# Moving loads, sums and a score spread in a two-layer graph kernel on one core

## The chip, the core and the metric

The kernel runs on one core of a Trainium2 chip. The metric is device time in microseconds (us) of one launch. A core has five engines that run their own instruction streams and wait for each other by semaphores: TensorE (PE in the profile, with its weight loads as PEld), VectorE (DVE), ScalarE (ACT), GpSimd (POOL) and SyncE (SP). Here SP only issues DMA transfers; GpSimd issues some of them too, and adds. All engines work on SBUF; matrix products land in the eight PSUM banks `a1, b1, c1, e1` (set 1) and `a2, b2, c2, e2` (set 2).

## What is computed

128 graphs of 128 nodes with 512 features each, all in float32, go through two layers. Cut to what matters:

```python
h = relu(layernorm(x))
# layer 0
Xw = h @ Wv + bv;  sj = Xw @ aw[:d, 0];  si = Xw @ aw[d:, 0]
e = leaky_relu(sj[:, None, :] + si[:, :, None] + ab[0], 0.2)
t = adj * exp(e);  t = t / (sum(t, -1) + 1e-12)
H = 0;  Xk = h
for k in range(3):
    H = H + Xk @ Wk[k] + bk[k]
    Xk = t @ Xk
x1 = x + relu(H)
# layer 1
h = relu(layernorm(x1))
q, k = split(h @ Wqk);  v = h @ Wv1
w = sum(q * (adj @ (k * mask)), -1) * mask / sqrt(512)
out = x1 + softmax(w, over the nodes)[:, :, None] * v
```

The query and key weights are folded into one matrix beforehand, so layer 1 needs two products of h: one for the score and one for v.

## The kernel before

Layer 0 takes two graphs at a time (64 pairs `p`). Its products are done by a Strassen scheme with seven products instead of eight (`strassen`). In one iteration stand: `y10(p)` (the products with Wk[1] and Wk[0], into set 1), `inner` and `outer` (the multiplications by the transition matrix and the sum x1), `y2(p + 2)` (the product with Wk[2], into set 2), `norm2(p)` (layer 1's norm, sent through DRAM to be transposed by 32x32 blocks), and, inside `y10`, `between`: the norm of x three pairs ahead and the transposes and left sums two pairs ahead (`begin`).

`behind(what, op, ...)` places an instruction after a named earlier one in its engine's stream without a wait of its own.

```python
def load_x(p, queue=nc.sync):
    xg[p] = loads.tile([P, G, D], FP, name="xg")          # 4 buffers
    queue.dma_start(xg[p], x[p * G:(p + 1) * G].rearrange("b n d -> n b d"))
...
def strassen(banks, left, right, s, first, ends, steps={}, gate="warm"):
    ...
    product(a, 1, first);  nc.scalar.copy(b, a)
    product(e, 5, first);  done["s"] = behind(gate, nc.scalar.copy, s[:, 0], e).ins
    product(b, 6);         done["u2"] = behind("s", nc.scalar.copy, c, b).ins
    product(a, 2);         ends[0, 0](a)
    product(c, 7);         nc.scalar.copy(s[:, 1], c);  ends[1, 1](e, s[:, 1])
    product(b, 3);         ends[0, 1](b, s[:, 0])
    product(c, 4);         ends[1, 0](c)
...
for p in range(NP):
    def between():
        ...
        if p + 2 < NP:
            behind("t", begin, p + 2)
        if p + 3 < NP:
            behind("left", norm0, p + 3)
    if p > 1:
        behind("x1", attention, p)
    y10(p, {1: between, 6: lambda: t_transposed(p)})
    if p > 0:
        behind("c12", for_layer1, p - 1)
    ...
    z = inner(p)
    if p == 0:
        y2(1); begin(2); spread_columns(1); behind("left", attention, 1)
    behind("c12" if p else "left", outer, p, z)           # ends with x1's store on SP
    ...
    if p + 2 < NP:
        y2(p + 2)
    ...
    norm2(p)                                              # h2d store and hv loads on SP
    if p + 4 < NP:
        load_x(p + 4)
    if p + 3 < NP:
        load_adj(p + 3)
    if p == 2:
        rightl = behind("x1", combine, ...)               # layer 1's weight sums, 4 large
    if 3 <= p < 3 + len(FACTORS):
        behind("x1", prepare, FACTORS[p - 3], stage)      # 4 small and their stores
```

In `y10` the ends of blocks (1,1) and (0,1) are DVE additions into PSUM (L85 in the profile), placed behind `rs`, the last result of the norm's statistics.

Layer 1 takes four graphs at a time (32 quads `q`). A Strassen scheme is used inside another: seven outer factors of seven products each, done in rounds of one or two factors. `put` and its forms `dve, act, pool, sync, swdge` keep each engine's stream in program order; `swdge` is a DMA issued by GpSimd.

```python
def spread_scores(col):
    t = small.tile([P, S32], FP, name="pwt", bufs=1)
    dve(nc.vector.transpose, t, col)
    d = dram.tile([S32, Q, S32], FP, name="pwd")
    sync(d.rearrange("g q b -> q g b"), t)
    dst = back[3].tile([P, 2 * G, N], FP, name="pw")
    sync(dst.rearrange("p g n -> p (g n)"), bcast(d, 0, 2 * G * N))
    return dst
...
def add_x1(q, pair):                                      # adds x1 to the values while loading
    swdge(values(q, pair), X1D[2 * q + pair].rearrange("g n d -> n g d"), accum_op=OP.add)
...
def catch_up(q):
    if q + 1 < NQ:
        load_left(q + 1, sync)
    scores(q - 1, 1, C[q - 1][:, 2])
    PW[q - 1] = spread_scores(W[q - 1])
    if q > 1:
        add_x1(q - 2, 0)

def last_block(q):                                        # block C22 of the outer scheme
    pool(nc.gpsimd.tensor_add, outer(q, 1), outer(q, 3), outer(q, 1))
```

`scores` multiplies and sums on DVE (the tile `junk`), the scores go through DRAM to be spread over all partitions (`pwd`, `pw`), then DVE takes the peak, ACT the exponentials and DVE the factors of the softmax; ACT scales the values with them.

The last quad (q = 31; prior = 30, late = 29):

```python
together(one_round(q, set1, (1, 6), ...), one_round(q, set2, (2, 7), ...),
         {2: lambda: scale(late, 1, 0), 3: lambda: scale(late, 1, 1), 4: prior_peaks,
          5: prior_factors, 6: lambda: [scale(prior, 0, j) for j in range(G)]})
add_x1(late, 1)
add_x1(prior, 0)
dve(nc.vector.tensor_add, outer(q, 3), outer(q, 3), outer(q, 1))
dve(nc.vector.tensor_add, outer(q, 1), outer(q, 0), outer(q, 1))
aggregate(q)                                              # four PE groups, ACT copies to agg
for j in range(G):
    scale(prior, 1, j)
add_x1(prior, 1)
for at in ((late, 0), (late, 1), (prior, 0), (prior, 1)):
    store(*at)
scores(q, 0, c[:, 2])
# then r4, r5, r3: rounds of one factor, interleaved, with the last quad's own softmax
```

Of the kernel before, what the change touches and what calls it, by code (L numbers as in the profile page):

```python
# [1 line left out]

# [13 lines left out]
def kernel(  # L16
# [32 lines left out]
    G = 2  # L49
# [400 lines left out]
    def attention(p):  # L450

        a, y, pz = ag.pop(p), Y2[p], PZ.pop(p)
        z = front.tile([P, G, N], FP, name="z", bufs=1)
        for j in range(G):
            nc.vector.tensor_scalar(z[:, j, :], pz[:, j, :], y[:, j, 1, HD:], cz, op0=OP.add, op1=OP.add)  # L455
        nc.vector.scalar_tensor_tensor(z, z, 0.2, z, op0=OP.mult, op1=OP.max)
        done["z"] = nc.scalar.activation(z, z, AF.Exp).ins
        d = small.tile([P, 2, G], FP, name="d")
        for j in range(G):
            nc.vector.scalar_tensor_tensor(z[:, j, :], z[:, j, :], 1.0, a[:, j, :], op0=OP.mult,  # L460
                                           op1=OP.mult, accum_out=d[:, 0, j:j + 1])
        nc.vector.tensor_scalar(d[:, 0], d[:, 0], 1e-12, None, op0=OP.add)
        nc.vector.reciprocal(d[:, 1], d[:, 0])
        t = T[p] = front.tile([P, G, N], FP, name="t", bufs=1)
        for j in range(G):
            done["t"] = nc.vector.tensor_scalar(t[:, j, :], z[:, j, :], d[:, 1, j:j + 1], None,
                                                op0=OP.mult).ins
        aT = front.tile([P, G, N], FP, name="aT", bufs=1)
        nc.vector.transpose(aT.rearrange("p g n -> p (g n)"),  # L469
                            agb.pop(p).rearrange("p g q i -> p (g q i)"))  # L470
        for j in range(G):
            b = p * G + j
            behind("z", nc.scalar.activation, aT[:, j, :], aT[:, j, :], AF.Copy, scale=maskT[:, b:b + 1])
        nc.sync.dma_start(ATD[p], aT)
# [59 lines left out]

    RWD = {o: dram.tile([P, 7, HD], FP, name=f"rwd{o}", bufs=1) for o in FACTORS}
# [90 lines left out]
# [3 lines that stand above are left out]
                behind("t", norm0, 2)  # L629
                behind("rs", begin, 1)  # L630
                return
            if p + 2 < NP:
                behind("t", begin, p + 2)
            if p + 3 < NP:
                behind("left", norm0, p + 3)

# [12 lines left out]
        if p == 0:  # L649
            y2(1)  # L650
            begin(2)
            spread_columns(1)
            behind("left", attention, 1)
        behind("c12" if p else "left", outer, p, z)
        if p == 0:
# [11 lines left out]
        if p + 4 < NP:  # L667
            load_x(p + 4)
        if p + 3 < NP:
            load_adj(p + 3)  # L670
        if p == 2:
            rightl = behind("x1", combine, {(kh, k): rl[:, kh * HC:(kh + 1) * HC, k] for kh in range(2)
                              for k in range(2)}, [tl[:, i] for i in range(4)])
        if 3 <= p < 3 + len(FACTORS):
            behind("x1", prepare, FACTORS[p - 3], stage)
# [152 lines left out]
    def spread_scores(col):  # L828
# [5 lines left out]
        sync(d.rearrange("g q b -> q g b"), t)  # L834
        dst = back[3].tile([P, 2 * G, N], FP, name="pw")
        sync(dst.rearrange("p g n -> p (g n)"), bcast(d, 0, 2 * G * N))
# [35 lines left out]
    def catch_up(q):  # L872

        if q + 1 < NQ:
            load_left(q + 1, sync)
        scores(q - 1, 1, C[q - 1][:, 2])
        PW[q - 1] = spread_scores(W[q - 1])
        if q > 1:
            add_x1(q - 2, 0)

    def last_block(q):

        pool(nc.gpsimd.tensor_add, outer(q, 1), outer(q, 3), outer(q, 1))
# [11 lines left out]
    EARLY, LATE = FACTORS[:4], FACTORS[4:]  # L895
    sums = inner_sums(0, LATE)
# [59 lines left out]
    last_block(prior)  # L956
    soft = {}

    def prior_peaks():
        soft[0] = peaks(W[prior], PW.pop(prior))  # L960
        exp_own(*soft[0])
        for j in range(2):
            exp(*soft[0], j)

    def prior_factors():
        for j in range(2, 2 * G):
            exp(*soft[0], j)
        factors(*soft[0])
# [6 lines left out]
             {2: lambda: scale(late, 1, 0), 3: lambda: scale(late, 1, 1), 4: prior_peaks,  # L975
              5: prior_factors, 6: lambda: [scale(prior, 0, j) for j in range(G)]})
    add_x1(late, 1)
    add_x1(prior, 0)

    dve(nc.vector.tensor_add, outer(q, 3), outer(q, 3), outer(q, 1))  # L980
    dve(nc.vector.tensor_add, outer(q, 1), outer(q, 0), outer(q, 1))
    aggregate(q)
    for j in range(G):
        scale(prior, 1, j)
    add_x1(prior, 1)
    for at in ((late, 0), (late, 1), (prior, 0), (prior, 1)):
        store(*at)
    scores(q, 0, c[:, 2])

# [4 lines left out]
    r5 = one_round(q, set2, (5,), s2, plain_ends(lambda i, j: c[:, 2:3, i, j]))  # L994
# [16 lines left out]

    def steps(*order):
        for round, i in order:
            round[i]()

    steps((r4, 0), (r4, 1), (r5, 0), (r4, 2), (r5, 1), (r4, 3))
# [6 lines left out]
    steps((r4, 6))  # L1023
    scores(q, 1, c[:, 0])
# [7 lines left out]

    dve(nc.vector.tensor_add, outer(q, 1), outer(q, 1), outer(q, 2))
    exp(*soft[1], 1)
    dve(nc.vector.tensor_add, outer(q, 3), outer(q, 3), outer(q, 2))
    factors(*soft[1])
    steps((r3, 3), (r3, 4))
    finish(1, 0, c[:, 3, 0], nc.sync)
    steps((r3, 5))
    finish(1, 1, c[:, 3, 1], nc.scalar)  # L1040
    finish(0, 0, c[:, 1, 0], nc.sync)
# [27 lines left out]
```

## Time and profile before

| | |
|---|---|
| time, median of 3 | 2317.68 us (2314.05 to 2321.01) |
| span of the profiled run | 2333.3 us |
| PE busy | 2247.4 us (96%) |
| DVE busy | 1679.4 us (72%) |
| ACT busy | 1254.2 us (54%) |
| POOL busy | 690.4 us (30%) |
| DMA moved | 507.77 MB, mean 218 GB/s |

In the profile `L90` is the line that issues nearly every matrix product and `L554` the helper through which layer 1 issues its work, so in layer 1 an instruction is told by its tiles, written `out<-in`. A square bracket at a line's end tells how long the engine was idle before it and what ended the idling. Layer 0 runs to about 1510 us, layer 1 from there, and the last quad's end from about 2270.

### The profile page before, as it was taken

The page shows a single profiled execution, that of the slowest core. Times are in us where ns is not written, and L with a number is a line of the kernel's source. Part 1 is how long each engine was busy: PE and PEld are TensorE (multiplying, and loading weights), DVE is VectorE, ACT ScalarE, POOL GpSimd, SP SyncE. Part 2 cuts the span into 40 slices and gives each one's busy share as a digit, 9 for nine tenths or more (in the row PEclk, how much of TensorE's full clock was granted, in tenths as well). Part 3 has the DMA queues.
Part 4 walks back from the last instruction along what each step waited for, and adds up shares of the span by engine and source line. Part 5 has one row for each costly group of instructions (what it writes and reads, how often), then busy time and mean ns, then how long its engine had stood idle before and what let it go on. Part 6 is the DMA issues. An engine that isn't in the chain of part 4 may idle for free.

```text
span 2333.3 us, 28894 instructions
## 1 busy us (share of the span) xinstructions
PE 2247.4 (96%) x8227; PEld 1549.4 (66%) x8227; DVE 1679.4 (72%) x4466; ACT 1254.2 (54%) x2932; POOL 690.4 (30%) x787
## 2 busy tenths in 40 slices
PE   8899999999999999999999999999999999999996
PEld 5565655666665665666656566578877878878774
DVE  5577667676766766667666676578877878878776
ACT  3445554554555555455555455446665656656664
POOL 2112111211211211121121121245555555555552
PEclk9999999999999999999999999999999999999998
DMA  8577686766767766666676675768787878878886
GB/s 211 151 240 250 200 265 204 234 200 205 236 200 206 241 202 195 212 217 201 212 225 201 205 241 172 257 207 233 225 237 221 237 222 236 236 216 233 239 221 159
DMA packets 343502, 507.77 MB, mean 218 GB/s; under 512 B 33178, under 2 KB 198426, under 8 KB 326958
## 3 DMA queue, kind: packets, MB, share of 16 engines
q1 hardware_dynamic: 302060, 382.40, 52.9%
q0 software_dynamic: 40992, 123.00, 19.6%
q8 instruction: 65, 1.06, 0.2%
q14 instruction: 95, 0.78, 0.1%
q10 hardware_dynamic: 290, 0.53, 0.1%
HBM read 289.62 MB, written 216.18 MB: 217 GB/s over the span
## 4 chain that ended last, share of the span: by engine, by line
PE 55%; DMA 18%; DVE 15%; ACT 8%; issue 2%; SPq 1%; POOL 1%; DVEq 0%; POOLq 0%; ACTq 0%
PE c L90 16%; PE a L90 15%; PE b L90 14%; DMA xg<-in_x_dram 9%; PE e L90 9%; ACT h L305 4%; DMA pw<-pwd 3%; DMA pwd<-pwt 3%; DVE junk L554 3%; DVE st L281 2%; DVE c L554 1%; DVE s L554 1%; DMA h2d<-h 1%; DVE wcol L554 1%; DVE fw L411 1%
## 5 line engine op out<-in xcount | busy, mean ns | idle before, releaser
L554 POOL TENSOR_TENSOR c<-s,c 128x512 f32<-128x512 f32 (+1 forms) x186 | 200.0, 1090 | 377.8 <-DVE s L554 372.9
L110 POOL DMA_DIRECT2D agb<-in_adj_dram x256 | 150.2, 592 | 531.8 <-DVE aT L469 407.4
L90 PE MATMUL a<-r,x 128*128 128x512 f32 x512 | 243.6, 598 | 3.6 <-ACT a L487 3.5
L554 DVE SCALAR_TENSOR_TENSOR junk<-agg,wscale,c 128x512 f32<-128x512 f32 x128 | 198.0, 1547 | 30.9 <-POOL c L554 25.6
L90 PE MATMUL b<-rw,in 128*128 128x256 f32 x896 | 216.2, 381 | 1.2 <-ACT b L554 1.2
L90 PEld LDWEIGHTS b<-rw,in 128*128 128x128 f32 x896 | 171.1, 191 | 25.7 <-ACT b L554 2.3
L554 POOL TENSOR_TENSOR c<-c 128x1024 f32<-128x1024 f32 x62 | 159.4, 2572 | 2.9 <-DVE c L554 0.7
L281 DVE BATCH_NORM_STATS2 st<-xg 128x6 f32<-128x512 f32 x128 | 82.3, 685 | 82.4 <-DMA xg<-in_x_dram 81.8
L90 PEld LDWEIGHTS a<-r,x 128*128 128x128 f32 x512 | 93.2, 192 | 69.7 <-issue 62.5
L90 PE MATMUL c<-t,x 128*128 128x512 f32 x256 | 125.2, 612 | 13.7 <-ACT s L385 13.3
L90 PE MATMUL a<-w,x 128*128 128x257 f32 x512 | 132.3, 380 | 3.1 <-DVE z L455 3.1
L90 PE MATMUL b<-w,sx 128*128 128x257 f32 x512 | 132.6, 381 | 0.0
L554 ACT ACTIVATE c<-c,wcol 128x512 f32<-128x512 f32 x124 | 86.2, 720 | 83.3 <-DVE wcol L554 83.3
L85 DVE TENSOR_TENSOR e<-e,s 128x512 f32<-128x512 f32 x64 | 44.7, 698 | 119.9 <-ACT s L385 119.9
L305 ACT ACTIVATE h<-xg,rs 128x512 f32<-128x512 f32 x128 | 97.2, 806 | 56.8 <-DVE rs L293 56.7
L90 PE MATMUL c<-rw,in 128*128 128x256 f32 x448 | 110.7, 387 | 16.9 <-ACT c L554 16.9
L377 ACT COPY b<-a 128x257 f32<-128x257 f32 (+1 forms) x128 | 59.5, 465 | 123.4 <-PE a L90 120.6
L90 PE MATMUL c<-t,sx 128*128 128x512 f32 x256 | 121.3, 596 | 2.3 <-ACT c L85 2.1
L90 PE MATMUL b<-t,sx 128*128 128x512 f32 x256 | 120.6, 593 | 0.0
L90 PE MATMUL b<-r,sx 128*128 128x512 f32 x256 | 120.3, 592 | 0.0
L90 PE MATMUL e<-t,sx 128*128 128x512 f32 x256 | 120.3, 592 | 0.0
L90 PE MATMUL a<-rw,f 128*128 128x256 f32 x448 | 108.9, 382 | 9.7 <-ACT agg L554 9.4
(243 smaller groups left out, 5172.5 us busy)
## 6 DMA issues: line engine op xcount, KB each, us to landing
fd<-fw POOLq DMA_DIRECT2D x62, 1024.0 KB, 6.7
x1d<-x SPq DMA_DIRECT2D x64, 512.0 KB, 7.0
h2d<-h SPq DMA_DIRECT2D x64, 512.0 KB, 3.5
hv<-h2d SPq DMA_DIRECT2D x256, 128.0 KB, 3.8
f<-fd SPq DMA_DIRECT2D x32, 1024.0 KB, 9.4
xg<-in_x_dram SPq DMA_DIRECT2D x63, 512.0 KB, 4.7
hd<-h SPq DMA_DIRECT2D x63, 512.0 KB, 3.1
hv<-hd SPq DMA_DIRECT2D x252, 128.0 KB, 2.9
```

Source lines behind the costliest of these rows:

```text
L85: return op(*args, **how)
L90: done["mm"] = op(*args, **how).ins
L110: nc.gpsimd.dma_start(agb[p][c * S32:(c + 1) * S32].rearrange("p g q i -> p (g q) i"), v[c])
L281: nc.vector.bn_stats(st, src[:, j, :])
L305: nc.scalar.activation(to, at, AF.Relu, bias=rs[:, 1, j:j + 1], scale=rs[:, 0, j:j + 1])
L377: nc.scalar.copy(b, a)
L411: nc.vector.transpose(blocks[:, k, j].rearrange("p f (n b) -> p f n b", n=Q), hv[:, j].rearrange("p n (k f a) -> p k f n a", k=2, f=HC)[:, k])
L554: done[engine] = op(*args, **how).ins
```

## The change

The change moves work; the arithmetic is the same but for who does it at the end.

- In layer 0, `load_x(p + 4)` is issued right behind x1's store, ahead of norm2's store and loads in SP's stream. It is for having x in SBUF when the statistics want it.
- Layer 1's weight sums (`combine`, `prepare`) leave the place ahead of attention and go behind the norm's statistics in `between`.
- In the first iteration, attention's first step (z) goes ahead of `begin(2)`.
- In layer 1, the score spread is issued by GpSimd instead of SP, the accumulation of x1 ahead of it, and block C22 waits, by way of a copy of one column into `gate`, for DVE's inner sums of the next quad. It is for letting DVE's scores run without GpSimd's addition beside them.
- At the end, the prior quad's softmax goes behind `aggregate`, its values are scaled on ACT, added to a loaded copy of x1 (`xp`) on GpSimd, and stored from there (`finish_scaled`); the sums with factor 5's product go to GpSimd in pieces, and one of the four last finishes goes to ACT and GpSimd.

```diff
-    def attention(p):
+    def attention(p, early_work=None):
...
-            nc.vector.tensor_scalar(z[:, j, :], pz[:, j, :], y[:, j, 1, HD:], cz, op0=OP.add, op1=OP.add)
-        nc.vector.scalar_tensor_tensor(z, z, 0.2, z, op0=OP.mult, op1=OP.max)
+            done["pz"] = nc.vector.tensor_scalar(z[:, j, :], pz[:, j, :], y[:, j, 1, HD:], cz,
+                                                 op0=OP.add, op1=OP.add).ins
+        if early_work:
+            behind("pz", early_work)
+        behind("left" if early_work else "pz", nc.vector.scalar_tensor_tensor, z, z, 0.2, z, op0=OP.mult, op1=OP.max)
...
@@ between()
                 behind("left", norm0, p + 3)
+            if p == 2:
+                rightl.update(behind("rs", combine, ...))
+            if 3 <= p < 3 + len(FACTORS):
+                behind("rs", prepare, FACTORS[p - 3], stage)
...
             y2(1)
-            begin(2)
             spread_columns(1)
-            behind("left", attention, 1)
+            attention(1, lambda: begin(2))
         behind("c12" if p else "left", outer, p, z)
+        if p + 4 < NP:
+            load_x(p + 4)
...
         norm2(p)
-        if p + 4 < NP:
-            load_x(p + 4)
         if p + 3 < NP:
             load_adj(p + 3)
-        if p == 2:
-            rightl = behind("x1", combine, ...)
-        if 3 <= p < 3 + len(FACTORS):
-            behind("x1", prepare, FACTORS[p - 3], stage)
...
@@ spread_scores
-        sync(d.rearrange("g q b -> q g b"), t)
+        swdge(d.rearrange("g q b -> q g b"), t)
         dst = back[3].tile([P, 2 * G, N], FP, name="pw")
-        sync(dst.rearrange("p g n -> p (g n)"), bcast(d, 0, 2 * G * N))
+        swdge(dst.rearrange("p g n -> p (g n)"), bcast(d, 0, 2 * G * N))
...
@@ catch_up
             load_left(q + 1, sync)
+        if q > 1:
+            add_x1(q - 2, 0)
         scores(q - 1, 1, C[q - 1][:, 2])
         PW[q - 1] = spread_scores(W[q - 1])
-        if q > 1:
-            add_x1(q - 2, 0)

     def last_block(q):

+        if q + 2 < NQ:
+            o = LATE[0]
+            pool(nc.gpsimd.tensor_copy, gate, IN[q + 1, o][:, 3, :1])
         pool(nc.gpsimd.tensor_add, outer(q, 1), outer(q, 3), outer(q, 1))
...
@@ the last quad
     last_block(prior)
+    xp = back[3].tile([P, 2, G, D], FP, name="xp")
+    for i in range(2):
+        sync(xp[:, i], X1D[2 * prior + i].rearrange("g n d -> n g d"))
...
-             {2: lambda: scale(late, 1, 0), 3: lambda: scale(late, 1, 1), 4: prior_peaks,
-              5: prior_factors, 6: lambda: [scale(prior, 0, j) for j in range(G)]})
+             {2: lambda: scale(late, 1, 0), 3: lambda: scale(late, 1, 1)})
     add_x1(late, 1)
-    add_x1(prior, 0)
...
+    soft[2] = peaks(W[prior], PW.pop(prior))
     aggregate(q)
-    for j in range(G):
-        scale(prior, 1, j)
-    add_x1(prior, 1)
-    for at in ((late, 0), (late, 1), (prior, 0), (prior, 1)):
-        store(*at)
+    exp_own(*soft[2])
+    for j in range(2 * G):
+        exp(*soft[2], j)
+    for pair in range(2):
+        store(late, pair)
     scores(q, 0, c[:, 2])
+    factors(*soft[2])
...
+    def sum_of_p5(end):
+        def both(*args, at):
+            end(*args)
+            for to in (1, 3):
+                pool(nc.gpsimd.tensor_add, c[:, to, at[0], at[1]], c[:, to, at[0], at[1]], c[:, 2, at[0], at[1]])
+        return both
...
+    def finish_scaled(quad, pair, graphs, at, r):
+        w = 3 * 2 * G + pair * G
+        for j in range(graphs.start, graphs.stop):
+            v = C[quad][:, at, j].rearrange("p h d -> p (h d)")
+            act(nc.scalar.activation, v, v, AF.Copy, scale=W[quad][:, w + j:w + j + 1])
+        v = C[quad][:, at, graphs].rearrange("p j h d -> p j (h d)")
+        pool(nc.gpsimd.tensor_add, r[:, pair, graphs], r[:, pair, graphs], v)
+        ...                                               # store on SP
+    finish_scaled(prior, 0, slice(0, G), 0, xp)
     steps((r4, 0), (r4, 1), (r5, 0), (r4, 2), (r5, 1), (r4, 3))
...
     steps((r4, 6))
+    finish_scaled(prior, 1, slice(0, G), 1, xp)
     scores(q, 1, c[:, 0])
...
-    dve(nc.vector.tensor_add, outer(q, 1), outer(q, 1), outer(q, 2))
     exp(*soft[1], 1)
-    dve(nc.vector.tensor_add, outer(q, 3), outer(q, 3), outer(q, 2))
     factors(*soft[1])
     steps((r3, 3), (r3, 4))
+    finish_scaled(q, 1, slice(1, 2), 3, x1)
     finish(1, 0, c[:, 3, 0], nc.sync)
     steps((r3, 5))
-    finish(1, 1, c[:, 3, 1], nc.scalar)
-    finish(0, 0, c[:, 1, 0], nc.sync)
+    finish(0, 0, c[:, 1, 0], nc.scalar)
     steps((r3, 6))
     finish(0, 1, c[:, 1, 1], nc.scalar)
```

More of the change, by code (lines that the diff above doesn't have):

```diff
@@ L1 @@
 from contextlib import ExitStack
+from functools import partial
 import concourse.bass as bass
@@ L533, in norm2 @@
         HV2[p] = by_blocks(norm_relu(X1[p], rs=statistics(X1[p], "u2")), H2D[p])
+    rightl = {}
     RWD = {o: dram.tile([P, 7, HD], FP, name=f"rwd{o}", bufs=1) for o in FACTORS}
@@ L635, in between @@
                 behind("left", norm0, p + 3)
+            if p == 2:
+                rightl.update(behind("rs", combine, {(kh, k): rl[:, kh * HC:(kh + 1) * HC, k]
+                                                     for kh in range(2) for k in range(2)},
+                                     [tl[:, i] for i in range(4)]))
+            if 3 <= p < 3 + len(FACTORS):
+                behind("rs", prepare, FACTORS[p - 3], stage)
         if p > 1:
@@ L666 @@
         norm2(p)
-        if p + 4 < NP:
-            load_x(p + 4)
         if p + 3 < NP:
             load_adj(p + 3)
-        if p == 2:
-            rightl = behind("x1", combine, {(kh, k): rl[:, kh * HC:(kh + 1) * HC, k] for kh in range(2)
-                              for k in range(2)}, [tl[:, i] for i in range(4)])
-        if 3 <= p < 3 + len(FACTORS):
-            behind("x1", prepare, FACTORS[p - 3], stage)
         if p == 3 + len(FACTORS):
@@ L895 @@
     EARLY, LATE = FACTORS[:4], FACTORS[4:]
+    gate = small.tile([P, 1], FP, name="gate", bufs=1)
     sums = inner_sums(0, LATE)
@@ L956 @@
     last_block(prior)
+    xp = back[3].tile([P, 2, G, D], FP, name="xp")
+    for i in range(2):
+        sync(xp[:, i], X1D[2 * prior + i].rearrange("g n d -> n g d"))
     soft = {}
[L959 to L968, printed above, removed]
     together(one_round(q, set1, (1, 6), s1, plain_ends(lambda i, j: c[:, 0:2, i, j])),
@@ L974 @@
                  lambda i, j: c[:, 0:1, i, j].to_broadcast([P, 2, HD]), True)),
-             {2: lambda: scale(late, 1, 0), 3: lambda: scale(late, 1, 1), 4: prior_peaks,
-              5: prior_factors, 6: lambda: [scale(prior, 0, j) for j in range(G)]})
+             {2: lambda: scale(late, 1, 0), 3: lambda: scale(late, 1, 1)})
     add_x1(late, 1)
-    add_x1(prior, 0)
     dve(nc.vector.tensor_add, outer(q, 3), outer(q, 3), outer(q, 1))
     dve(nc.vector.tensor_add, outer(q, 1), outer(q, 0), outer(q, 1))
+    soft[2] = peaks(W[prior], PW.pop(prior))
     aggregate(q)
-    for j in range(G):
-        scale(prior, 1, j)
-    add_x1(prior, 1)
-    for at in ((late, 0), (late, 1), (prior, 0), (prior, 1)):
-        store(*at)
+    exp_own(*soft[2])
[3 more added lines that the diff above has]
+        store(late, pair)
     scores(q, 0, c[:, 2])
+    factors(*soft[2])
     r4 = one_round(q, set1, (4,), s1, adding_ends(lambda i, j: c[:, 0:1, i, j],
                                                   lambda i, j: c[:, 3:4, i, j], True))
-    r5 = one_round(q, set2, (5,), s2, plain_ends(lambda i, j: c[:, 2:3, i, j]))
+    def sum_of_p5(end):
[4 more added lines that the diff above has]
+        return both
+    ends5 = plain_ends(lambda i, j: c[:, 2:3, i, j])
+    r5 = one_round(q, set2, (5,), s2, {at: partial(sum_of_p5(end), at=at) for at, end in ends5.items()})
     r3 = one_round(q, set1, (3,), s1, adding_ends(lambda i, j: c[:, 1:2, i, j],
@@ L1010, in finish @@
         queue.dma_start(out[(2 * q + pair) * G + j], r)
+    def finish_scaled(quad, pair, graphs, at, r):
[5 more added lines that the diff above has]
+        pool(nc.gpsimd.tensor_add, r[:, pair, graphs], r[:, pair, graphs], v)
+        first = (2 * quad + pair) * G
+        nc.sync.dma_start(out[first + graphs.start:first + graphs.stop].rearrange("b n d -> n b d"),
+                          r[:, pair, graphs])
     def steps(*order):
```

## Prediction

> **What bounds the kernel now.** I read the page first, then the busy time by stage, then what TensorE (PE) itself waited for, and last three stretches of the timeline. The page's slices:
>
> ```profile
> PE   8899999999999999999999999999999999999996
> ...
> PEclk9999999999999999999999999999999999999998
> ```
>
> PE is busy nearly everywhere, so nothing that DVE, ACT or the queues save counts until it closes a hole in PE's row. The stages (columns: stretch, its length, then busy time and instructions of PE, PEld, DVE, ACT, POOL, then clock, DMA share, GB/s):
>
> ```profile
> 70.00:250.00 180.00, 169.89 (x556) 105.97 (x557) 128.43 (x419) 91.80 (x217) 30.26 (x52) 0.97 0.68 209
> 250.00:1510.00 1260.00, 1234.33 (x4142) 773.48 (x4141) 865.17 (x2819) 649.88 (x1551) 229.94 (x390) 0.99 0.70 217
> 1510.00:2270.00 760.00, 741.84 (x3173) 602.23 (x3172) 607.48 (x1050) 458.85 (x1035) 396.30 (x295) 1.00 0.80 228
> 2270.00:2333.30 63.30, 41.37 (x163) 30.55 (x161) 42.97 (x84) 28.08 (x77) 17.08 (x13) 0.87 0.59 154
> ```
>
> PE's idle time is 10.1 + 25.7 us in layer 0, 18.2 us in layer 1 and 21.9 us in the last 63 us. The last stretch also ran at 0.87 of the clock: 0.13 x 63.3 = 8 us more. That is all there is to win, and some of it (the very last finishing chain, about 6 us) can't go. PE's own list of waits names the holes:
>
> ```profile
> PE c L90 <- ACT c L554: 16.9, 14, 4.8
> PE c L90 <- ACT s L385: 14.5, 21, 2.4
> PE a L90 <- ACT agg L554: 9.4, 1, 9.4
> PE a L90 <- DVE t L466: 8.6, 5, 2.7
> PE e L90 <- DVE e L85: 7.8, 5, 3.2
> ```
>
> The first and third belong to layer 1, the others to layer 0. What stands behind each is seen in the timeline. Layer 0, iteration near 250 us:
>
> ```profile
> 255.28 1.29 DVE L281 BATCH_NORM_STATS2 st<-xg 128x6 f32<-128x512 f32 x2 [4.26 <-DMA xg<-in_x_dram]
> ...
> 276.34 0.69 PE L90 MATMUL a<-ident,t 128*128 128x128 f32 x2 [2.66 <-DVE t L466]
> 276.82 3.06 PE L90 MATMUL a<-r,x 128*128 128x512 f32 x4
> ```
>
> x is issued only behind norm2's h2d store (at 248.61 in the same timeline), lands some 6.6 us later, and DVE has stood still for it 4.26 us. The statistics, ACT's r and the additions into PSUM (L85) then run late, and PE's last product waits. The other pair shows the price of a hole: after 2.66 us of idling the next four records took 3.06 us, where the same group elsewhere takes 1.88.
>
> **What the Trainium skill says.** "TensorE: Matmul & The Clock Gate", section "What's actually happening": an idle PE falls to half clock, and a window of about 3.4 us passes before it is back. The trace agrees in kind: the holes of 2.07 us and more (near 92, 224, 273, 353, 931, 979, 1542, 2300 us) are followed by slow groups; at half speed for 3.4 us each costs an estimated 1.7 us on top. Holes of 1 us aren't. "SBUF — State Buffer", section "SBUF: two separate sides": DVE with two SBUF inputs and a GpSimd operation share a port pair, and "whichever" starts first keeps it "for the whole instruction". The trace agrees that one of the two stands still for the whole of the other (layer 1 below); who starts first is not what its start times show. "DMA: Bandwidth & Descriptors", section "Two DMAs through the same engine are not ordered": in one queue descriptors start in order. So a small transfer queued behind a large one waits for it; in this trace the score spread's store was issued at 1531.50 behind two 1 MB loads of the same queue, and what waits for it left at 1539.30, 7.8 us later, against 3.9 to 5.4 in the quads after 2000 us.
>
> **The change, part by part.**
>
> *x behind x1's store.* The buffer of xg is free at the same moment as x1's store, so the load can leave at once: near 250 us the store went out at 242.27 and xg at 248.61, 6.3 us earlier; in most iterations it is 4 to 6. DVE waits 81.8 us in all for xg (43 times, 5.2 at most), mean 1.9, so nearly all of it goes. On PE's side that is c <- ACT s (14.5 less 1.15 of the first iteration's other cause) and three of the five waits for e (5.3): 18.7 us, with three re-clockings (353, 931, 979 us) 3 x 1.7 = 5.1, together 23.8. I take 80%: **19 us**.
>
> *Weight sums behind the statistics.* Now four 128x256 operations (0.39 to 0.42 us) sit between norm2's statistics and attention in seven iterations, and the four of 1.14 us once; t comes late, and PE waits (7.0 us in layer 0 after 70 us), with two re-clockings 10.4 us. They move behind rs, just ahead of the additions into e and b. There they can hold PE's next product: at 285.30 PE used e one record after DVE had finished it at 284.3, so a 1.6 us block in front would cost some 0.7 us in each of seven iterations, and the 4.6 us block once about 3. 8 us gained less 5 to 6: **3 us**.
>
> *begin(2) inside attention(1).* PE waited 3.1 us for z near 67 us, since DVE first waited for hv and did the transposes and sums. With z first, only the transposes (1.3 us) remain ahead of y2's first product, so PE starts at about 68.3 instead of 70.34: **2.5 us** with part of a re-clocking.
>
> *Layer 1's scores.* One quad:
>
> ```profile
> 2050.05 0.69 DVE L554 TENSOR_REDUCE peak<-pw 128x4 f32<-128x512 f32 x1 [4.88 <-DMA pw<-pwd]
> ...
> 2061.04 4.05 DVE L554 SCALAR_TENSOR_TENSOR junk<-agg,wscale,c 128x512 f32<-128x512 f32 x1 [0.81 <-POOL c L554]
> 2061.72 2.81 POOL L554 TENSOR_TENSOR c<-c 128x1024 f32<-128x1024 f32 x1
> ```
>
> The score (junk) takes 4.05 us instead of 0.75, because GpSimd's C22 addition holds the port. With C22 held back behind the gate, scores are ready 3.3 us sooner. Then pwd and pw went through SP: issued 2066.16 and 2070.01, read at 2074.6. If the 3.3 us stayed whole, DVE's 118.9 us of waiting for pw (31 times, mean 3.8) would nearly go, and with it ACT's late exponentials and PE's 16.9 us (at 2053.23 PE had idled 1.69 us for ACT). But they don't quite stay. On GpSimd's queue the spread stands behind x1's 512 KB accumulation (issued 2060.94, landing 8.8 us in the median), so pwd would land at about 2069.5 where it now lands at 2070.0, and a GpSimd issue takes 1.2 us for a large transfer and 0.6 for a small one instead of 0.33. I expect pw about 1 us earlier in a usual quad. In the first quad, which has no accumulation ahead, the 4.8 us hole and its slow clock (some 3.4 us lost) should go whole. GpSimd meanwhile sits in a wait for pwd, so C22 and the next additions come 2 to 3 us later and may hold DVE's second pair of scores. Of 18.2 + 3.4 us I take a little over half: **12 us**.
>
> *The end.* The hole there:
>
> ```profile
> 2304.67 0.69 DVE L554 TENSOR_REDUCE peak<-pw 128x4 f32<-128x512 f32 x1 [8.02 <-DMA pw<-pwd]
> ...
> 2309.65 1.22 PE L90 MATMUL a<-rw,f 128*128 128x256 f32 x2 [9.40 <-ACT agg L554]
> ```
>
> ACT's copies of agg stood behind the prior quad's exponentials, those behind pw. Now agg is copied first, so PE goes on from 2300.3 with three products (4 us at most). But the prior's scaling on ACT is put ahead of ACT's first copy of r4. With scores 3.3 us sooner and pw at about 2299.8, DVE reaches the peak at 2301.8 (its two 128x1024 additions of 1.24 us come first), ACT's four exponentials end at 2304.4, factors at 2304.9, two scalings (1.36) at 2306.3: PE then waits some 5 us for r4's copy. So the hole is halved, and three products stand in front of it: about 5 us. Behind it DVE loses the two 128x1024 additions (2.4 us) and one finish (0.75), given to GpSimd and ACT; GpSimd gets eight small and three large additions, whose port hold returns some of it. **8 us**, from 2 to 14.
>
> **Sum.** 19 + 3 + 2.5 + 12 + 8 = 44.5 us of the profiled run. The timed runs are 15.6 us shorter than the profiled one with the same work, so a seventh of the waiting isn't there: 44.5 x 0.86 = 38 us, which gives **2279 us**, 1.7% less.
>
> **Rivals.** (1) GpSimd's queue as the new wait: pwd stays behind the accumulation until after 2070, pw lands at 2076 or later, and C22's successors hold DVE. DVE is already close behind PE in layer 1 (607 of 760 us, and DVE, the score spread and ACT stand in the chain that ended last there), so 1 us in each of 30 quads might be lost in place of layer 1's gain: 2279 + 10 + 30, about 2320 us. For it: in layer 0 GpSimd waits up to 6.6 us for a 1 KB store (pzd) of the same queue. Against: the accumulation moves ahead and no longer meets C22. (2) The early x load only feeds DVE, and PE's holes stay because ACT's static order is what delays them: layer 0 gives 5 us, the total 2295. Against it: the holes carry xg in the chain. (3) Everything works and the holes close: about 38 + 20 + 15 us less, 2250.
>
> **Range and chances.** 2254 to 2306 us. 2% faster means under 2271.3; that needs all three stages to deliver, or layer 1 to give nearly all. Faster by over 2%: 0.33; within 2%: 0.64; slower by over 2%: 0.03.
>
> **What would show it.** DVE's wait for xg falls from 81.8 to under 15 us; PE's c <- ACT s in layer 0 to under 4; no score over 1 us except where another GpSimd addition runs; pw read in about 1 us less after the score than its gain of 3.3 would give; one hole of about 5 us near 2302 in place of 9.4. Wrong if DVE's wait for peak grows, if PE waits newly for e behind the weight sums by more than 1 us each, or if the last stretch after PE's restart is as long as now (23.7 us).

## The result: 5% slower, and where layer 1's quads lost it

The changed kernel takes 2440.73 us (median of 4 runs, 2435.05 to 2442.70) against 2319.35 us of the kernel before in the same comparison: ratio 1.0522, 95% interval 1.0494 to 1.0549. The prediction was 2279 us. All ratios below are against runs of the kernel before on the same chip at the same time; microseconds worked out from a ratio use that comparison's median of before (2319 to 2330 us).

The busy row and the clock row of the page after, in 40 slices:

```profile
PE   9899999999999999999999999989999899898896
...
PEclk9999999999999999999999999999999999999998
```

The last third, all nines before, now has eights. The stages (columns as before: stretch, length, busy time of PE, PEld, DVE, ACT, POOL, then clock, DMA share, GB/s):

```profile
250.00:1510.00 1260.00, 1217.81 (x4107) 765.96 (x4106) 874.19 (x2795) 650.32 (x1537) 227.37 (x388) 1.00 0.67 214
1510.00:2270.00 760.00, 686.35 (x2795) 540.75 (x2794) 517.88 (x921) 403.79 (x917) 386.29 (x337) 0.97 0.69 201
2270.00:2437.80 167.80, 136.32 (x544) 105.99 (x542) 115.89 (x209) 83.56 (x196) 81.61 (x72) 0.94 0.64 184
```

PE's idle time in the 760 us of layer 1 went from 18.2 to 73.7 us, with 2795 matmul records in place of 3173, at 0.97 of the clock in place of 1.00. For a comparison of equal work, both traces are cut at the first score of layer 1 and run to the end. Before, then after:

```profile
1508.90:2333.30 824.40, 784.31 (x3337) 633.27 (x3335) 651.55 (x1133) 487.63 (x1112) 414.48 (x308) 0.99 0.79 223
```

```profile
1510.10:2437.80 927.70, 822.58 (x3337) 646.68 (x3335) 633.74 (x1130) 487.34 (x1113) 467.80 (x409) 0.96 0.69 198
```

The same 3337 records take 103.3 us more: 65.0 us of new idle time (40.1 before, 105.1 after) and 38.3 us more busy time. The lower clock (0.986 before and 0.964 after, unrounded) accounts for an estimated 22 us of that at most: 3.6% of 927.7 us less 1.4% of 824.4. The rest isn't explained by the granted clock. DVE's busy time fell. Layer 0 reaches its end 1.2 us later than before (6.6 if the slow start of before's profile, told of below, is taken off). So nearly all of the loss is in layer 1 and the end, and layer 0's expected gain is missing as well. PE's waits after:

```profile
PE c L91 <- ACT c L559: 64.8, 29, 4.2
PE b L91 <- ACT b L378: 33.4, 25, 1.7
PE b L91 <- ACT b L559: 17.9, 17, 5.9
PE a L91 <- DVE c L559: 9.1, 16, 1.0
PE e L91 <- DVE e L86: 8.9, 3, 5.3
```

The first was 16.9 us before; the second (layer 0) wasn't in the list at all; the third was 1.2 and the fourth 0.3. From the list of all engines' waits:

```profile
POOL pw L559 <- DMA pwd<-pwt: 228.7, 29, 8.8
DVE peak L559 <- DMA pw<-pwd: 194.7, 30, 7.6
```

GpSimd now stands still 7.9 us in each quad for the spread's own store, and DVE's wait for the weights grew from 118.9 to 194.7 us. One quad after, in the timeline:

```profile
2076.17 1.19 POOL L559 DMA_DIRECT2D c<-x1d  x1
...
2077.86 0.21 DVE L559 STREAM_TRANSPOSE pwt<-wcol 128x32 f32<-128x32 f32 x1
...
2078.37 0.74 POOL L559 DMA_DIRECT2D pwd<-pwt  x1 [1.00 <-DVE pwt L559]
...
2087.15 0.58 POOL L559 DMA_DIRECT2D pw<-pwd  x1 [8.03 <-DMA pwd<-pwt]
...
2087.87 2.36 POOL L559 TENSOR_TENSOR c<-c 128x1024 f32<-128x1024 f32 x1
...
2090.19 2.49 POOL L559 TENSOR_TENSOR c<-s,c 128x512 f32<-128x512 f32 x2
...
2091.52 0.69 DVE L559 TENSOR_REDUCE peak<-pw 128x4 f32<-128x512 f32 x1 [6.51 <-DMA pw<-pwd]
...
2092.71 2.94 DVE L559 SCALAR_TENSOR_TENSOR junk<-agg,wscale,c 128x512 f32<-128x512 f32 x1
...
2092.75 2.35 POOL L559 TENSOR_TENSOR c<-c 128x1024 f32<-128x1024 f32 x1
...
2095.00 1.56 PE L91 MATMUL c<-rw,in 128*128 128x256 f32 x6 [2.17 <-ACT c L559]
```

The store pwd is issued 2.2 us behind the accumulation; its load pw can only be issued at 2087.15, and all of GpSimd's work behind it in its stream (C22 at 2087.87, then three more additions) starts then. The last of these meets the score that follows the peak, `scores(q, 0)`, at 2092.71, and that score takes 2.94 us. This is the first pair of a quad's scores; the one that C22 held in the kernel before is the second pair, in front of pwt (31 of its 32 long scores), and the gate did free it: none of the 30 long scores after is one. ACT's exponentials wait for the peak, its copy of b stands behind them, and PE idles 2.17 us. From one quad's transpose of the weights (pwt) to the next is 28.7 us in the median, before 25.2; over all 30 such steps that is 103 us more.

PE's hole is where the loss shows, not where it is made. The chain of work that ended last (columns: start, us, what) leaves PE in nearly all of these quads and runs in a circle:

```profile
2078.37 8.23 DMA pwd<-pwt
...
2087.93 4.76 POOL c L559 x3
...
2092.71 2.96 DVE junk L559 x2
```

From there it goes over DVE's sums to the next quad's scores, pwt and store. It passes 27 of the stores: behind 17 of them it goes on as here, through GpSimd's stalled stream, and behind the other 10 through pw's landing and the peak. So the standing still and the late weights both stand in it.

Layer 0's new wait, in the iteration near 392 us of the changed kernel:

```profile
392.50 1.28 DVE L282 BATCH_NORM_STATS2 st<-x 128x6 f32<-128x512 f32 x2
...
396.52 0.43 DVE L433 TENSOR_TENSOR y<-e,s 128x257 f32<-128x257 f32 x1 [2.74 <-ACT s L386]
...
396.98 0.43 DVE L434 TENSOR_TENSOR y<-b,s 128x257 f32<-128x257 f32 x1
397.32 0.24 DVE L283 BATCH_NORM_AGGREGATE mv<-st 128x2 f32<-128x6 f32 x2
...
400.26 1.50 ACT L306 ACTIVATE h<-x,rs 128x512 f32<-128x512 f32 x2
...
401.96 0.57 ACT L378 COPY b<-a 128x512 f32<-128x512 f32 x1
...
402.59 1.98 PE L91 MATMUL b<-t,sx 128*128 128x512 f32 x4 [1.35 <-ACT b L378]
```

The statistics are done at 393.8, but their aggregation stands in DVE's stream behind y's two additions, which wait for ACT's s until 396.5. So ACT's norm (h) comes late, the copy of a behind it too, and PE's product into b waits. In the kernel before, the aggregation stands ahead of y's additions in all but one iteration; after, it stands behind them in every second iteration from pair 12 on, 25 times. The program text of neither was touched: the compiler orders the stream.

### The profile page after: what moved, and what is told of

Read it like the earlier page. It is cut to its first block, busy times and chain, and to the rows that moved or that the text cites. A ratio compares the mean times of both kernels' runs of the same rounds, so it can differ in the third digit from the quotient of the medians.

```text
span 2437.8 us, 28862 instructions
## 1 busy us (share of the span) xinstructions
PE 2277.2 (93%) x8227; PEld 1557.8 (64%) x8227; DVE 1680.9 (69%) x4463; ACT 1259.8 (52%) x2933; POOL 743.5 (30%) x888
## 5 line engine op out<-in xcount | busy, mean ns | idle before, releaser
L91 PE MATMUL b<-rw,in 128*128 128x256 f32 x896 | 230.4, 399 | 18.0 <-ACT b L559 17.9
L91 PEld LDWEIGHTS b<-rw,in 128*128 128x128 f32 x896 | 177.6, 201 | 53.9 <-ACT b L559 27.9
L91 PE MATMUL c<-rw,in 128*128 128x256 f32 x448 | 124.5, 422 | 64.9 <-ACT c L559 64.8
L559 DVE SCALAR_TENSOR_TENSOR junk<-agg,wscale,c 128x512 f32<-128x512 f32 x128 | 160.8, 1256 | 30.7 <-POOL c L559 25.2
L559 DVE TENSOR_REDUCE peak<-pw 128x4 f32<-128x512 f32 x31 | 21.3, 686 | 194.7 <-DMA pw<-pwd 194.7
L91 PE MATMUL b<-t,sx 128*128 128x512 f32 x256 | 123.0, 603 | 33.4 <-ACT b L378 33.4
L559 POOL TENSOR_TENSOR c<-c 128x1024 f32<-128x1024 f32 (+1 forms) x70 | 151.7, 2170 | 3.5 <-DVE c L559 0.8
L91 PEld LDWEIGHTS c<-rw,in 128*128 128x128 f32 x448 | 89.8, 207 | 89.6 <-ACT c L559 77.3
```

The lines of the kernel that those rows point to most:

```text
L91: done["mm"] = op(*args, **how).ins
L559: done[engine] = op(*args, **how).ins
```

## The experiments

Two causes are to be told apart in layer 1. The queue theory (Q): pwd lands late because it goes through GpSimd's queue behind the accumulation. The stall theory (S): lateness alone has slack; what costs is that GpSimd stands still in its own stream. For layer 0 the order theory (O): the order of DVE's stream, not the load of x, makes the new wait.

**e1: the spread back on SP.** Both DMAs of the spread, nothing else:

```diff
-        swdge(d.rearrange("g q b -> q g b"), t)
+        sync(d.rearrange("g q b -> q g b"), t)
         dst = back[3].tile([P, 2 * G, N], FP, name="pw")
-        swdge(dst.rearrange("p g n -> p (g n)"), bcast(d, 0, 2 * G * N))
+        sync(dst.rearrange("p g n -> p (g n)"), bcast(d, 0, 2 * G * N))
```

> The changed kernel, but the score spread is issued by SP again; C22 stays held back, the accumulation of x1 stays ahead. Theory Q (the spread's 16 KB store stands behind the 512 KB accumulation in GpSimd's one DMA queue): the store lands within 6 us instead of 8.5, a quad takes 25 to 26 us instead of 28.9, the whole 2330 to 2360 us. Rival H (the held-back C22 and the additions behind it block DVE's second pair of scores, whoever issues the spread): a quad stays at 27.5 us or more, the whole over 2400 us.

Measured: 2329.65 us, ratio 1.0014 (0.9996 to 1.0032). The whole loss of layer 1 is gone. Yet the spread isn't quick here: on SP it stands behind the next quad's factor load, pw is issued 7.4 us after pwd in the median, and from the end of pwt to the peak are 12.2 us, against 9.2 in the kernel before and 13.5 in the changed one. The quad's period is 25.1 us. So Q's time came true without the quick landing that it names. Weights that come 3 us later than before make this kernel no slower than before; that they take away what the gate gives is seen in e8.

**e2: the spread ahead of the accumulation**, both still on GpSimd:

```diff
-        if q > 1:
-            add_x1(q - 2, 0)
         scores(q - 1, 1, C[q - 1][:, 2])
         PW[q - 1] = spread_scores(W[q - 1])
+        if q > 1:
+            add_x1(q - 2, 0)
```

> The changed kernel, but in GpSimd's stream the spread (store and load) goes ahead of the accumulation of x1, still on GpSimd's queue. Theory Q: the store lands in 2 to 4.5 us, GpSimd's wait for it falls from 228.7 us to about 100, the whole 2330 to 2365 us. Rival P (GpSimd's queue is slow for such a transfer whatever stands ahead): landing stays near 8 us, the whole over 2420 us.

Measured: 2402.11 us, ratio 1.0328 (1.0308 to 1.0348): some 45 us came back by the ratios, of the 76 to 111 expected. GpSimd's wait for pwd fell to 155.9 us, not to 100. It lies between Q and P. A quad of it:

```profile
2083.65 0.74 POOL L559 DMA_DIRECT2D pwd<-pwt  x1 [2.14 <-DVE pwt L559]
2089.85 0.59 POOL L559 DMA_DIRECT2D pw<-pwd  x1 [5.46 <-DMA pwd<-pwt]
...
2091.33 2.88 POOL L559 TENSOR_TENSOR c<-c 128x1024 f32<-128x1024 f32 x1
...
2094.01 0.69 DVE L559 TENSOR_REDUCE peak<-pw 128x4 f32<-128x512 f32 x1 [3.71 <-DMA pw<-pwd]
...
2096.68 2.94 DVE L559 SCALAR_TENSOR_TENSOR junk<-agg,wscale,c 128x512 f32<-128x512 f32 x1
```

The store now lands in 5.6 us (median; 8.3 in the changed kernel), and the peak comes 10.6 us after pwt: sooner than in e1. Still the period is 27.5 us, 2.4 more than e1's, since GpSimd stalls 5.4 us a quad, C22 starts at 2091.33 and the score is held 2.94 us as in the changed kernel (31 of 128 scores, again the first pair). That speaks against Q as the main cause, and for S.

**e5: only the load issued by SP.** The store stays on GpSimd behind the accumulation; the second line of e1's edit alone.

> The changed kernel with the spread's store left on GpSimd's queue behind the accumulation, but its broadcast load (pw) issued by SP, so that GpSimd no longer stands still between the two. The store still lands some 8.5 us after its issue. Theory S (it is GpSimd's standing still in its stream that costs, since C22 and the next two additions come late and meet DVE's scores): most of layer 1's loss goes, 2345 to 2370 us, and pwd's landing stays above 8 us. Rival L (it is the late weights themselves, whoever issues them): GpSimd's wait for pwd is gone, but DVE's wait for the peak stays near 195 us and the time stays above 2410 us.

Measured: 2332.08 us, ratio 1.0007 (0.9991 to 1.0023), better than S had said. One line of code takes back 1.0522 - 1.0007 = 5.15%, some 119 us; between the two traces it is 107 us. From the first score to the end:

```profile
1509.50:2330.30 820.80, 786.73 (x3337) 634.43 (x3335) 560.02 (x1130) 488.49 (x1113) 450.38 (x378) 0.99 0.78 224
```

and a quad of its timeline:

```profile
2062.08 0.73 POOL L559 DMA_DIRECT2D pwd<-pwt  x1 [1.01 <-DVE pwt L559]
...
2063.95 2.37 POOL L559 TENSOR_TENSOR c<-c 128x1024 f32<-128x1024 f32 x1
...
2066.45 2.50 POOL L559 TENSOR_TENSOR c<-s,c 128x512 f32<-128x512 f32 x2
...
2069.11 0.32 SPq L559 DMA_DIRECT2D pw<-pwd  x1
2069.36 2.35 POOL L559 TENSOR_TENSOR c<-c 128x1024 f32<-128x1024 f32 x1 [0.41 <-DVE c L559]
...
2073.52 0.69 DVE L559 TENSOR_REDUCE peak<-pw 128x4 f32<-128x512 f32 x1 [4.31 <-DMA pw<-pwd]
...
2074.32 0.75 DVE L559 SCALAR_TENSOR_TENSOR junk<-agg,wscale,c 128x512 f32<-128x512 f32 x1
```

The store waits for the accumulation as before (pw goes out 7.0 us after pwd), and the peak is still 12.5 us after pwt in the median. But C22 runs at 2063.95, 1.9 us after pwd in place of 9.5, the last of the additions is over at 2071.7, and the score takes 0.75 us. Of all 128 scores one takes over 1.5 us here, against 30 in the changed kernel and 32 in the one before. DVE's wait for the peak is 149.4 us, still more than the 118.9 of the kernel before. The rival L (late weights cost, whoever issues them) expected over 2410 us and falls. One detail of S's expectation was off: the store lands in 7.2 us, not over 8, so the weights come 1.0 us sooner than in the changed kernel. If that counted in full in each of 29 quads, it would be 29 of the 107 us (an estimate); the rest belongs to the standing still.

**e3: the aggregations held ahead of y's additions** on DVE, in the changed kernel (the norm's statistics are traced before the product y2, and y2's two additions placed behind them):

```diff
+        mv2 = moments(X1[p])                 # bn_stats, bn_aggr; done["mv"]
         if p + 2 < NP:
             y2(p + 2)
...
-            (1, 1): lambda e, t: nc.vector.tensor_add(y[:, 1, 1], e, t),
-            (0, 1): lambda b, t: nc.vector.tensor_add(y[:, 0, 1], b, t),
+            (1, 1): lambda e, t: after_mv(nc.vector.tensor_add, y[:, 1, 1], e, t),
+            (0, 1): lambda b, t: after_mv(nc.vector.tensor_add, y[:, 0, 1], b, t),
```

> The changed kernel, but in layer 0 the two aggregations of norm2's statistics are put ahead of y2's two additions in DVE's stream, as they stood before the change; nothing else. Theory O (in every second iteration the new order of DVE's stream makes the aggregation wait for y2's end, so h and then ACT's copy b<-a are late, and PE waits 1.35 us): PE's wait for ACT b (33.4 us) falls under 3, the whole is 30 to 45 us shorter than the changed kernel, about 2400. Rival X (the earlier x load itself, by DMA traffic or by DVE taking the statistics earlier, causes that hole): it stays, 2430 to 2445 us.

Measured: 2421.51 us, ratio 1.0412 (1.0397 to 1.0428), some 1.1% or 25 us below the changed kernel by the ratios, 19 us by the medians, less than the 30 to 45 expected. PE's wait for b fell from 33.4 to 16.0 us (26 times 0.6), not to nothing: half of it has another cause (e12).

**e4: layer 1's quads as before**, so layer 0's moves and the end alone (e1's edit, no gate, the accumulation behind the scores again).

> The changed kernel with the three edits of layer 1's quads undone (spread on SP, accumulation behind it, no gate): layer 0's moves and the end alone. If all of the loss is layer 1's spread and the order O costs what the x load gains, about 2310 to 2325 us; if layer 0 or the end lose of themselves, 2335 or more.

Measured: 2334.74 us, ratio 1.0030 (1.0014 to 1.0047). Layer 0's moves and the end together, predicted to give 32.5 us, cost 7, with the 33.4 us wait for b standing in layer 0.

**e6: begin(2) inside attention(1) alone**, in the kernel before.

> The kernel before with one edit alone: begin(2) inside attention(1). The edit's own instructions run once, before 75 us. Theory O (the compiler's order of DVE's instructions in the later iterations flips with any edit of layer 0: y's additions ahead of norm2's aggregations, in every second iteration): PE's wait for b behind ACT's copy appears with some 33 us, and the time is 15 to 30 us above the kernel before. Rival (the hole comes with the early x load or with the moved weight sums): no such wait, and the time within 4 us of the kernel before.

Measured: 2325.47 us, ratio 0.9978 (0.9966 to 0.9991). No wait for b; DVE's order in the later iterations is that of the kernel before. So O in the form "any edit of layer 0 turns the order" falls: this one doesn't.

**e7 and e9: the early load of x alone**, in the kernel before, with the order held as in e3 (e7) and left to the compiler (e9):

```diff
         behind("c12" if p else "left", outer, p, z)
+        if p + 4 < NP:
+            load_x(p + 4)
...
         norm2(p)
-        if p + 4 < NP:
-            load_x(p + 4)
```

> The kernel before with the early x load alone, and with norm2's aggregations forced ahead of y's additions on DVE, as they stand in the kernel before. Predicted worth of the early x load: 19 us of a profiled span, 16 of a timed run. If that was right: 15 to 20 us below the kernel before, DVE's wait for xg under 15 us, PE's c <- ACT s under 4. If the rival of the prediction was right (x only feeds DVE): 5 us or less below.

> The kernel before with the early x load alone, DVE's order left to the compiler. It puts y's two additions ahead of norm2's aggregations in every second iteration here, as in the changed kernel (not so in the run with begin(2) in attention(1) alone). Theory O2 (that order is the cause of the new hole, and the early x load brings the order about): PE's wait for b behind ACT's copy comes to some 33 us against 15 with the order held, y's order is the changed kernel's, and the time is 14 to 20 us above the run with the order held, about 2335 us or ratio 1.000 to 1.004. Rival (the hole needs the moved weight sums as well): no more than 16 us of that wait, and the same time as with the order held, ratio 0.995.

Measured: e7 2318.43 us, ratio 0.9949 (0.9922 to 0.9977); e9 2344.15 us, ratio 1.0080 (1.0054 to 1.0106). PE's wait for b, in e7 and then in e9:

```profile
PE b L90 <- ACT b L382: 15.3, 25, 0.6
```

```profile
PE b L90 <- ACT b L377: 33.1, 25, 1.4
```

In e9 the aggregations stand behind y's additions in the same alternating pattern as in the changed kernel. The two programs differ only in the edit that holds that order, and the order costs 1.3%, 30 us by the ratios and 27 between the traces, more than was expected (18 us of it in this wait, 5 in PE's wait for t, 4 in PE's busy time behind the holes). In both, DVE's wait for xg, 80 to 85 us where x isn't moved, is 4.2 and 3.6 us.

**e10: layer 1's part without GpSimd's queue.** The kernel before with the gate on C22, and the spread kept on SP but ahead of the next quad's factor load:

```diff
-        if q + 1 < NQ:
-            load_left(q + 1, sync)
         scores(q - 1, 1, C[q - 1][:, 2])
         PW[q - 1] = spread_scores(W[q - 1])
+        if q + 1 < NQ:
+            load_left(q + 1, sync)
```

> The kernel before with layer 1's gate on C22, and the spread kept on SP but issued ahead of the next quad's factor load; nothing else. Predicted worth of layer 1's scores: 12 us of a profiled span, 10 timed. If the score held only by the port and the place in the queue matter: DVE's wait for the peak falls from 119 to under 50 us, PE's c <- ACT c from 17 to under 4, scores 0.75 us, and 14 to 22 us below the kernel before (ratio 0.990 to 0.994). If the factor load's delay costs as much: ratio 0.997 to 1.002.

Measured: 2300.87 us, ratio 0.9908 (0.9876 to 0.9939): 21 us less. DVE's wait for the peak and layer 1's stretch:

```profile
DVE peak L554 <- DMA pw<-pwd: 35.9, 29, 5.9
```

```profile
1503.00:2240.00 737.00, 735.67 (x3171) 601.69 (x3170) 550.17 (x1052) 464.61 (x1036) 400.98 (x326) 1.00 0.79 234
```

PE is idle 1.3 us in 737, and its wait for ACT's c (16.9 us before) isn't in the list any more. Layer 1 had the gain in it that the change was after. The two edits weren't run apart in this kernel; e1 against e8 below tells what the place in the queue is worth once the gate stands.

**e11: the end alone**, in the kernel before.

> The kernel before with the new end alone. Predicted: 8 us of a profiled span (7 timed), with one hole of some 5 us in front of r4's second group in place of 9.4. In the changed kernel that hole was 5.93 us and a second one of 3.91 us stood behind it. If the second hole belongs to the end itself: 2 to 4 us below the kernel before, ratio 0.998 to 0.999. If the late spread of the changed kernel caused it: 6 to 9 us below, ratio 0.996 to 0.9975, and no second hole over 1 us.

Measured: 2326.46 us, ratio 0.9997 (0.9973 to 1.0021), no difference to be seen. PE's holes there are 6.55 and 3.91 us; before, 9.40 and 1.56. The second hole belongs to the end itself.

**e8 and e12: what the parts give together.** e8 is the changed kernel with e3's order and e10's place of the spread. e12 moves, on top of it, the transpose and ACT's two scalings of aT (0.68 us ahead of the copy of a) behind the copy of e in y10's round:

```diff
-        y10(p, {1: between, 6: lambda: t_transposed(p)})
+        y10(p, {1: between, 6: lambda: (masked_adj(p, "s") if p > 1 else None, t_transposed(p))})
```

> The changed kernel with the aggregations ahead of y's additions, and with the spread back on SP and put ahead of the next quad's factor load there; the gate, the accumulation ahead of the scores, the moves in layer 0 and the end are kept. If the two causes are separate and add: the 19 us of the order and the 111 us of the queue together from 2441, which is 2311; and the spread ahead of the load should take its landing from 7.3 to about 3 us, worth another 0 to 15 us: 2295 to 2311. If the factor load's delay costs as much as the spread gains: 2310 to 2330.

> The best version so far (order held, spread on SP ahead of the factor load) with ACT's two scalings of aT and their transpose moved behind the copy of e in y10's round, so that the copy of a that PE's product into b waits for stands 0.6 us earlier. That wait was 16.0 us, 26 times 0.6. If it is a pure ACT order: the wait falls under 4 us and the time by 8 to 15 us to 2272 to 2279. If PE then waits for the next thing (the sums of x on DVE): 0 to 5 us less.

Measured: e8 2287.08 us, ratio 0.9803 (0.9780 to 0.9825); e12 2270.08 us, ratio 0.9771 (0.9747 to 0.9795). e8 is below the 2295 to 2311 us expected; e12 is 7 us below e8 by the ratios and 17 by the medians, where 8 to 15 had been expected. e12 beats the kernel before by 2.3% and the changed one by 7%. PE's wait for b fell from 16.0 to 1.1 us with it, so that it was ACT's order and nothing behind it.

In layer 1, e8 differs from e1 in one thing: the spread goes ahead of the factor load. The peak comes 9.4 us after pwt in place of 12.2, and DVE's wait for it, in e1 and then in e8, is

```profile
DVE peak L559 <- DMA pw<-pwd: 143.0, 31, 9.1
```

```profile
DVE peak L567 <- DMA pw<-pwd: 36.4, 30, 5.1
```

From the first score to the end e1 takes 820.0 us and e8 797.0 (e4, without the gate, 820.5). So 3 us of lateness cost 23 us: in e1 it had only eaten the gate's gain. The stages of e12:

```profile
250.00:1471.00 1221.00, 1213.54 (x4114) 767.90 (x4113) 870.72 (x2797) 655.23 (x1540) 225.80 (x384) 1.00 0.72 221
1471.00:2203.00 732.00, 730.08 (x3148) 597.32 (x3147) 545.24 (x1048) 460.50 (x1030) 396.47 (x323) 1.00 0.79 234
2203.00:2266.80 63.80, 48.08 (x188) 37.43 (x186) 46.24 (x83) 32.47 (x83) 28.79 (x24) 0.88 0.62 191
```

PE is idle 7.5 us in 1221 and 1.9 us in 732; what is left to win lies in the last 64 us.

## Why the prediction was wrong, step by step

**Layer 1's scores (12 us of gain, in truth over 100 of loss).** This is the step that failed. It saw that pwd would stand behind the accumulation in one queue, and put its landing at 2069.5, which is 6.6 us after an issue 3.3 us earlier than the 2066.16 of before. It landed 8.3 us after its issue in the median. That mistake is small. The large one is the sentence that GpSimd "meanwhile sits in a wait for pwd, so C22 and the next additions come 2 to 3 us later": the wait was 7.9 us a quad, C22 started 9.5 us after pwd's issue (1.9 in e5), and e5 shows that this standing still, and not the late weights, is most of the cost. The prediction booked the wait as a side effect inside a gain of 12 us; it is a term of its own, and with the weights' lateness it made each quad 3.4 us longer (103 us over 30 steps). The score's hold by GpSimd, which the gate did end for the second pair, came back in the first pair of the next quad (2.94 us in 30 quads); the prediction had feared it for the second.

The other half of the step, that scores free of C22 and an early spread are worth something, was right and undersized: e10 gave 21 us (14 to 29), where 10 timed had been taken.

The first rival (GpSimd's queue as the new wait) had most of the mechanism, the late store and C22's successors holding DVE, though not GpSimd's standing still, and the size wrong: "1 us in each of 30 quads" was 3.4, and so 3% for "slower" was far too low. It was set aside because the accumulation no longer meets C22, which is true and beside the point. As to where transfers wait: "DMA: Bandwidth & Descriptors", section "SWDGE vs HWDGE vs iDMA", of the Trainium skill says that transfers of GpSimd and of SP go through different queues of one DMA engine, which takes turns between them. No run here shows the turns themselves. What they show is that the 16 KB store took 5.6 us to land even with no accumulation ahead of it in its queue (e2), and that on SP ahead of the loads 4.2 us passed from pwd's issue to pw's (e12). The prediction's figure for that last step, "3.9 to 5.4 in the quads after 2000 us", is 3.5 to 5.9 in its trace; nothing hangs on it.

**x behind x1's store (19 us).** The mechanism was right: DVE's wait for xg fell from 81.8 to 6.3 us, PE's wait for ACT's s fell from 14.5 to 0.7 us. The size, with the order held, is 0.5%, 12 us (5 to 18), against 16 timed: right within its interval, although 15.3 us of new waiting for b are in it. What failed is that the order of DVE's stream was taken as given. The early load turned it, and e9 shows 19 us lost where 16 were to be won. The second rival (x only feeds DVE, and ACT's static order keeps PE's holes) is half right: the holes behind s went, but ACT's order made the 15.3 us for b, which e12 removed.

**Weight sums (3 us).** PE's wait for t fell from 8.6 to 1.6 us, as said. Neither the hole of about 3 us nor the 0.7 us in each of seven iterations appeared: the large sums run at 108 to 113 us and the small ones from 132 us on, and PE doesn't wait for e there. The hole of 5.3 us for e stands at 89.4 us, ahead of them all, and e6 has it (5.5 us at 89.2) without this move. This part wasn't run alone.

**begin(2) in attention(1) (2.5 us).** e6: 5 us (2 to 8). PE's wait for z (3.1 us) became 0.75 us for x. The price, which the prediction didn't have, is the hole for e just named, where 2.5 us stood before (95.0 us): DVE stands 8.2 us there waiting for hv, and e's addition comes behind that.

**The end (8 us).** Halved as predicted: three products in front, then one hole, "some 5 us", measured 5.93. But a loss was missed behind it. The changed kernel's end:

```profile
2413.84 1.22 PE L91 MATMUL b<-rw,in 128*128 128x256 f32 x2 [5.93 <-ACT b L559]
...
2421.10 2.34 POOL L559 TENSOR_TENSOR xp<-xp,c 128x1024 f32<-128x1024 f32 x1 [5.16 <-issue]
...
2421.20 2.79 DVE L559 SCALAR_TENSOR_TENSOR junk<-agg,wscale,c 128x512 f32<-128x512 f32 x1
...
2424.98 0.69 PE L91 MATMUL e<-ident,wcol 128*128 128x128 f32 x2 [3.91 <-DVE c L559]
```

The prior quad's addition, given to GpSimd, holds the score of the last quad for 2 us, and PE idles 3.91 us in place of 1.56. The prediction named that hold ("whose port hold returns some of it") and left it small. From PE's restart to the end are 24.0 us, before 23.7: the sign that it had named for "wrong". Alone the end changes the time by -0.03%, within -0.3 and +0.2%.

**The factor 0.86.** It rested on a profiled run of the kernel before that is 15.6 us longer than the timed ones. In that profile y2's first product came at 70.34 us; in e10 and e7, with the same work up to there, it came at 64.92 and 64.95. So 5 us belong to one slow start and to none of the waits that were counted. From that product to layer 1's first score, before's profile and e10's both take 1438.5 us, with 35.5 and 35.8 us of idle PE, and e10's profile lies within 2 us of its median: the waits of layer 0 are there in timed runs too, and no discount was due on them. For layer 1 and the end this stays open.

**The sum.** The parts run by themselves give 12 (e7) + 5 (e6) + 21 (e10) + 1 (e11) = 39 us, where 38 had been predicted for the whole. That is luck: single terms were off in both directions, the weight sums are not in it, and e7 and e10 are not the change as it stood (the order held, the spread on SP). What made 2279 into 2441 was not in the sum at all: GpSimd's stall, and DVE's order.

## What to carry to other kernels

An instruction that waits in an engine's stream costs what stands behind it: before a dependent pair (a store, and the load of what it stored) moves to an engine that also computes, list that engine's next work and who waits for it, or let an engine that only issues transfers do the load. Ask of a late transfer whether its reader has slack, and ask it again after each gain: 3 us more from store to read left this kernel no slower than before and yet cost 23 us of what the gate could give, while GpSimd's standing still cost most of 107. And compare each engine's instruction order after every edit, since a moved load can turn the order of instructions that the edit doesn't name.

## What the runs showed of the hardware

The same 16 KB store was seen in four settings: 4.2 us from its issue to that of its load on SP ahead of the factor loads (e12), 7.4 on SP behind one (e1), and from issue to landing 5.6 on GpSimd's queue when the last accumulation had landed 6 us before (e2) and 8.3 behind a 512 KB accumulation (after), where it landed 0.3 us behind it.

DVE's score and GpSimd's addition hold each other up, and the recorded starts don't tell which one waits: in the changed kernel and in e2 the score's start (2092.71, 2096.68) stands ahead of the addition's (2092.75, 2096.72), and it is the score that takes 2.94 us in place of 0.75, the addition its usual 2.35.

New idle time of PE came with about half as much new busy time for the same 3337 matmul records: 65.0 and 38.3 us in the changed kernel, the clock falling from 0.99 to 0.96, and 42.9 and 21.4 us in e2, the clock staying at 0.99. In these stretches the clock was granted at half 18 times in the changed kernel, 5 in e2 and 3 before, for 3.4 us or more. All but the one at each run's end stand at a hole in PE's row of 1.9 us or more; not every such hole has one (the 2.17 us at 2095.00 has none).

Open: what makes the compiler turn DVE's order; why the changed kernel's accumulations land later than those of e5, whose store lands 1.1 us sooner with the same queue order; and where the busy time comes from that the granted clock doesn't explain.
